# Gated graph network and graph attention on 64 graphs: one product in three passes, the end of the last graph in halves, and a new table of leads

## The chip, the core and the metric

The kernel runs on one core of a Trainium2 chip. The metric is device time in microseconds (us) from the start to the end of one execution. Time before the change: 1938.69 us, the median of three runs (1938.57 to 1942.45).

The core has several engines, each with its own queue of instructions. TensorE (PE in the profile) multiplies matrices: a weight load (LDWEIGHTS, shown as PEld) puts a 128 x 128 block into the array, and a matmul streams columns past it into a PSUM bank. VectorE (DVE), ScalarE (ACT) and GpSimd (POOL) work elementwise, SyncE (SP) issues the DMA transfers. An instruction starts when those ahead of it in its own queue have started and when the semaphores that it waits for are set.

## The reference

x holds 64 graphs of 256 nodes with 256 features each, adj the 64 adjacency matrices. Two layers, both behind a layer norm and a relu, are added to x:

```python
h = relu(layernorm(x))
A = (adj != 0)
for i in range(3):                        # gated network
    m = h @ weight[i]                     # per graph, 256x256 by 256x256
    aggr = A^T @ m                        # sum over the sources of each node
    r, z, n = GRU gates of (aggr @ w_ih.T + b_ih, h @ w_hh.T + b_hh)
    h = (1 - z) * n + z * h
x = x + h

h = relu(layernorm(x)) @ W.T              # graph attention
e = leaky_relu(h . a_left (rows) + h . a_right (columns), 0.2)
e = where(adj == 0, -1e9, e)
x = x + softmax(e) @ h
```

Everything is fp32, and so are the inputs and the output.

## The kernel before, in words

**Tiling.** Two graphs make a pair, so there are 32 pairs (`NPAIR`, `G` = 2), and most tiles are 128 partitions by 512 elements: 256 features or nodes in two blocks of 128 (`NB`, `DB` = 2), two graphs beside each other. In the gated network the features lie on the partitions, and the product of `weight[i]` with the input half of the gates is folded into one matrix per layer at the start (lines L680 and around), so a layer is a propagation by the adjacency matrix (L889) and then the gates.

**Three passes.** A product of fp32 tiles is made as a sum of three cheaper ones. `split16` (L718 to L726) splits one operand: ScalarE rounds it to a shorter fp32 form ("round", L718), VectorE subtracts that from the operand to get the remainder in 16 bits ("half", L720), and a scaled 16-bit copy of the operand is made too, by ScalarE if the operand lies in a bank (L723), else by VectorE (L726). The constant operand is split once at the start (`fac` for the rounded part, `low` for its 16-bit parts). The product is then fac x round, and two 16-bit products, summed in one bank. `limbs` (L736, L737) is the same split without the third copy, for the operand of the propagation. In the gates, `gate` (L750) issues six matmuls of 512 columns for each matrix: one in the fp32 form and two in 16 bits, for two blocks of features. The planner counts a change between the two forms as `SWITCH`, and `narrow` turns the order of the passes round, so that two products in a row meet in the same form.

**The gated step** of each block of 128 features, after the gates: tanh of r (L908), u (L913), u plus the n gate (L916), tanh (L918), tanh of z (L921), and three VectorE steps that give the new h (L925 to L929). L772 adds a bias to the gate nh. The new h is turned from features to nodes by the DMA's transpose (`dma_turn`: the transpose at L782, two gathers at L787) and put together by ScalarE (`join`, L795); in the first and the last pair TensorE turns it.

**Attention.** `norm_relu` (L810 to L823) makes the layer norm: statistics on VectorE, an epsilon (L815), a power on GpSimd (L817), a shift (L819), and two relus on ScalarE (L823). Then come products with a_left and a_right (L987), the row of right terms (by DMA, L996 and L999, or in the last two pairs by TensorE, L1008), the leaky relu (L1013), the mask (L1016), the row maximum (L1018), the exponentials with their sums (L1024), a scaling of the sums (L1032, `total`), the reciprocal (L1034), and the turn of the weights p. The order of products is then not the reference's: softmax(e) @ (h W^T) is made as (softmax(e) @ h) W^T. `mix` is the first product, in three passes up to pair 29 (L1053) and in plain fp32 in pair 30 (L1061); `project` is the one with W^T, in three passes up to pair 29 (L1072) and, in pair 30, in plain fp32 behind a copy of the bank (L1079, L1083). `out` (L1088) scales by the reciprocal and adds x, and one transfer of 256 KB stores the graph (L1091).

**The last pair** (31; `far` is false for it alone) does it the other way round: h is turned by TensorE (L1102), copied (L1105) and multiplied with W^T (L1110, copied at L1114). Then, for each graph and each block of 128 rows, come the exponentials (L1120), the reciprocal (L1123), the turn of p (L1128) and its copy (L1131), the product with the finished h W^T (`mix`, L1135: two matmuls of 256 columns in plain fp32), `out` (L1138) and a store of 128 KB (L1141).

**What sets the order.** Each operation is handed to a planner (`Plan`) with a name, its engine, an estimate of its time, and what it reads and writes. Buffers come from pools (28 "full", 22 "round", 40 "half", 8 PSUM banks and so on), and at most four pairs are open at a time. The planner gives each operation a priority, a due time less the latency of what follows, less its lead, and then again and again writes out the operation that can start first by its estimates, among equals the one with the lower priority value. The order on each engine's queue is thus fixed when the kernel is built. The leads are the table `LEAD`, one number per name; the prefixes "first", "pen", "late" and "last" name pairs 0, 29, 30 and 31, "of 0" and "of 1" the graphs of a pair where they are done one by one:

```python
o.stage, o.name, o.lead = self.stage, self.prefix + name, self.lead.get(name, 0)
if self.prefix:
    o.lead += self.lead.get(o.name, 0)
...
for o in self.ops:
    o.prio -= o.lead
...
if fits and (best is None or (t, o.prio, o.seq) < best[0]):
    best = ((t, o.prio, o.seq), o)
```

The diff's places in full, and what calls them:

Of the kernel before, what the change touches and what calls it, by code (L numbers as in the profile page):

```python
# [31 lines left out]
    "A": -600500, "A16": -500, "G 0": 165000, "G 1": 5500, "b_nh": 44500, "b_rz": -8000, "b_rz half": -20500,  # L32
    "back 0": -414000, "back 0 gather": -44000, "back 0 of 0": -9000, "back 0 of 1": -66000, "back 1": -646000,
    "back 1 gather": -4000, "back 1 of 0": 110000, "back copy 0": 188500, "back copy 1": 65500, "c0 0": 13500,
    "c0 1": -4000, "c0 d": 169000, "c1 0": -3500, "c1 1": 1000, "c1 d": 11000, "d add 0": 29000,
    "d add 0 of 1": -14500, "d add 1": 103000, "d add 1 of 0": 38500, "d mul 0": 21000, "d mul 0 of 0": 2000,
    "d mul 0 of 1": 35000, "d mul 1": 193000, "d mul 1 of 1": 1000, "d sub 0": -43000, "d sub 0 of 1": -20000,
    "d sub 1": -40000, "d sub 1 of 0": -13000, "d sub 1 of 1": -26000, "dot 0": 32000, "dot 1": 37000,
    "exps 0": -105000, "exps 0 0": -13000, "exps 0 1": -4000, "exps 1": 202000, "exps 1 1": 26500, "fill": 36000,
    "first A": -14500, "first A16": -18500, "first back 0": 107000, "first back 0 gather": 1500,  # L40
    "first back 1": -6500, "first back 1 gather": -15000, "first back copy 0": 76000, "first back copy 1": 16500,
    "first c0 0": 4000, "first c0 1": -20000, "first c0 d": 12000, "first c1 0": -14500, "first c1 1": 52000,
    "first c1 d": 43000, "first d add 0": 1000, "first d add 1": -14000, "first d mul 0": 1000,
    "first d mul 1": 29000, "first d sub 0": -16000, "first dot 0": 21000, "first dot 1": 2000,
    "first exps 0": -11500, "first exps 1": 36000, "first fill": 31000, "first g0 0": 16000, "first g0 d": 33000,
    "first g1 0": 38000, "first g1 1": 38500, "first g1 d": -116500, "first h0 0": 18500, "first h0 1": -263000,
    "first h1 1": 28000, "first hi 0": -30500, "first hi 1": 55500, "first in 0 eps": -60000, "first in 0 pow": 8000,
    "first in 0 relu": -11000, "first in 0 shift": 35500, "first in 0 stats": -201000, "first in 1 eps": -79500,
    "first in 1 pow": 21500, "first in 1 relu": 11500, "first in 1 shift": 57500, "first in 1 stats": 15500,
    "first in hi 0": 26500, "first in lo 0": 7500, "first in lo 1": -27000, "first leaky 0": 35500,  # L50
    "first line 0": 35000, "first line 1": -10500, "first lo 0": -500, "first lo 1": -7500, "first load": -5000,
    "first m0 1": 23500, "first m0 d": 3000, "first m1 0": 17000, "first m1 1": 3500, "first mask 0": 1000,
    "first mask 1": 5000, "first max 0": -4500, "first max 1": -5000, "first mid 0 eps": -14000,
    "first mid 0 pow": -32000, "first mid 0 relu": -49000, "first mid 0 shift": -6500, "first mid 0 stats": -69000,
    "first mid 1 eps": 98000, "first mid 1 pow": -8000, "first mid 1 relu": 88500, "first mid 1 shift": 9000,
    "first mid 1 stats": -90500, "first mix 0": -33000, "first nh 0 scale": 38000, "first nh 0 topF": -58000,
    "first nh 1 scale": 110000, "first nh 1 topF": 33000, "first ni 0 topF": 12000, "first ni 1 topF": 27500,
    "first out 0": -56500, "first p copy 0": -1000, "first p copy 1": 102000, "first p turn 0": 16000,
    "first p turn 0 gather": -25500, "first p turn 1": -5000, "first p turn 1 gather": 65500, "first p0 0": -16000,
    "first p0 1": 6500, "first p0 d": 17000, "first p1 0": -44000, "first p1 1": -4000, "first p1 d": -58500,  # L60
    "first project 0": -14000, "first prop 0": -8000, "first prop 1": 1000, "first r 0": 3500,
    "first r 0 topT": -42000, "first r 1": -57000, "first r 1 topF": 104000, "first recip": 10500,
    "first res 0": -50000, "first res 1": -16000, "first right 0": -10500, "first right 1": -122500,
    "first store": -16000, "first tanh 0": 41500, "first tanh 1": 4000, "first total": -3000, "first turn 1": -4500,
    "first turn copy 0": -5500, "first turn copy 1": 110500, "first u 0": -8000, "first u 1": -2000,
    "first u add 0": 25500, "first u add 1": 39500, "first w load full": -20000, "first z 0": 15500,
    "first z 0 topF": -14000, "first z 1": -13000, "g0 0": -41000, "g0 0 of 0": -59000, "g0 0 of 1": -29500,
    "g0 1": -26500, "g0 1 of 0": 1000, "g0 d": -97500, "g0 d of 0": 57000, "g0 d of 1": -14000, "g1 0 of 0": 28500,
    "g1 0 of 1": -9500, "g1 1": -5000, "g1 1 of 0": -128000, "g1 d of 1": -8000, "h copy 0": 27000, "h copy 1": 50000,
    "h turn 0": 9000, "h turn 1": -5500, "h0 0": -55500, "h0 0 of 0": -21000, "h0 0 of 1": 8000, "h0 1": -127000,  # L70
    "h0 1 of 0": -8000, "h0 1 of 1": -6000, "h0 d": -58500, "h0 d of 0": 50000, "h0 d of 1": 5000, "h1 0": 99500,
    "h1 0 of 0": -66500, "h1 0 of 1": 14000, "h1 1": 24500, "h1 1 of 0": 16000, "h1 1 of 1": 17500,
    "h1 d of 0": 51500, "h1 d of 1": 49500, "hW 0": 41500, "hW 1": -104000, "hW copy 0": -4000, "hi 0": 82000,
    "hi 0 of 0": 99000, "hi 0 of 1": 73000, "hi 1": -95500, "hi 1 of 0": 54500, "hi 1 of 1": 54000, "ident": -32500,
    "in 0 eps": 8000, "in 0 pow": 26500, "in 0 relu": 313500, "in 0 shift": 3000, "in 0 stats": 136000,
    "in 1 eps": 30000, "in 1 pow": -39500, "in 1 relu": 8000, "in 1 shift": -4000, "in 1 stats": 401500,
    "in hi 0": -175000, "in hi 1": 128000, "in lo 0": 30000, "last A": 56000, "last A16": 8000, "last back 0": 83500,
    "last back 0 of 0": 57500, "last back 0 of 1": 2000, "last back 1": 4000, "last back 1 of 0": -46500,
    "last d add 0": -8000, "last d add 0 of 0": -47000, "last d add 0 of 1": 6000, "last d add 1": -45000,
    "last d add 1 of 0": -8000, "last d add 1 of 1": -18000, "last d mul 0": -10000, "last d mul 0 of 0": -16500,  # L80
    "last d mul 0 of 1": -7000, "last d mul 1": -17500, "last d mul 1 of 0": -1000, "last d mul 1 of 1": -21000,
    "last d sub 0 of 0": -21000, "last d sub 0 of 1": -8000, "last d sub 1": 8000, "last d sub 1 of 0": -37000,
    "last d sub 1 of 1": -17000, "last dot 1": 48500, "last exps 0 0": 47000, "last exps 0 1": 138000,
    "last exps 1 0": 105000, "last exps 1 1": 3000, "last fill": 150000, "last g0 0": -8000, "last g0 0 of 0": 4500,
    "last g0 0 of 1": 1000, "last g0 1": 5500, "last g0 1 of 1": -2000, "last g0 d": -30500, "last g0 d of 1": 49500,
    "last g1 0": 53500, "last g1 0 of 0": 15500, "last g1 1 of 0": -9500, "last g1 1 of 1": -8000,
    "last g1 d": -33000, "last g1 d of 0": 153000, "last g1 d of 1": -23500, "last h copy 0": 13500,
    "last h turn 1": 6000, "last h0 0": 12000, "last h0 0 of 0": 146500, "last h0 0 of 1": -4000, "last h0 1": 70500,
    "last h0 1 of 1": 10000, "last h0 d": -8000, "last h0 d of 0": 2000, "last h0 d of 1": 65500, "last h1 0": 17000,
    "last h1 0 of 0": 8000, "last h1 0 of 1": 16000, "last h1 1": 7500, "last h1 1 of 0": -43000,  # L90
    "last h1 1 of 1": -13000, "last h1 d of 0": -16000, "last h1 d of 1": -15000, "last hW 1": 20500,
    "last hW copy 1": -81000, "last hi 0": -37500, "last hi 0 of 0": 4000, "last hi 0 of 1": 66000,
    "last hi 1": -4000, "last hi 1 of 0": 56500, "last hi 1 of 1": 24500, "last in 0 eps": -4500,
    "last in 0 pow": 6000, "last in 0 relu": 2000, "last in 0 shift": -44500, "last in 0 stats": -16000,
    "last in 1 eps": 5500, "last in 1 pow": -47000, "last in 1 relu": -63000, "last in 1 shift": -10500,
# [299 lines left out]
def tile_gated_gnn_then_gat(  # L395
# [77 lines left out]
    def parts(b):  # L473
        return b.t[:, :GN].rearrange("p (k d) -> p k d", k=2)
# [707 lines left out]
```

## Time and profile before

| | |
|---|---|
| median of three runs | 1938.69 us (1938.57 to 1942.45) |
| the profiled execution, its own time | 1937.01 us |
| its span, first to last instruction | 1935.2 us |
| TensorE's granted clock | 1.000 |
| plain fp32 product with W^T in pair 30 (L1083) | 16 records |
| three-pass product with W^T, all pairs up to 29 (L1072) | 4% of the chain |
| weight-load records | 10320, as many as matmuls |
| DMA | 240.25 MB, mean 124 GB/s |

The profile is one execution on the chip. A record of busy time belongs to one instruction. A matmul of plain fp32 leaves two records. The chain that ended last is followed back from the last instruction, at each step to what released it or to the instruction before it on its engine; its shares tell where the time of the span went. In a chain line the first number is the start in us, the second the length, then come the engine, the tile, the line and the number of instructions. In a line of TensorE's timeline, a group of matmuls is shown with start, length, line, the tile written and the tiles read, partitions and columns, and in brackets the idle time ahead of it and what ended it. "SPq" is SyncE's queue, "q" behind another engine's name likewise.

### The profile page before, as it was taken

To read this page: it belongs to the slowest core of one execution; us is meant where nothing else is said; L and a number is where in the kernel's file an instruction comes from. 1 tells how busy PE (TensorE), PEld (TensorE's weight loads), DVE (VectorE), ACT (ScalarE), POOL (GpSimd) and SP (SyncE) were. 2 spreads that over 40 slices of the span, in tenths; PEclk is the share of its full clock that TensorE was granted. 3 is DMA by queue.
4 is the path that set the end of the run, shared out by engine and by line. 5 is a ranking of instruction groups with operands and counts; after the bars stand their busy time and mean duration, and the time that the engine had idled before them with its cause. 6 is when DMAs were issued, how large, how long until landed. Compare 5 with 4: busy or idle time off the path is not lost.

```text
span 1935.2 us, 31695 instructions
## 1 busy us (share of the span) xinstructions
PE 1926.4 (100%) x10320; PEld 1215.5 (63%) x10320; DVE 1652.2 (85%) x3954; ACT 1608.7 (83%) x2798; POOL 196.8 (10%) x280
## 2 busy tenths in 40 slices
PE   9999999999999999999999999999999999999999
PEld 6556656666666666666666666666666666666668
DVE  7678888888888888898888898888988888888888
ACT  7668888888888888888888888888888888888876
POOL 3000101001011010110010110101100101100000
PEclk9999999999999999999999999999999999999999
DMA  4157766667756677766697566777666976666642
GB/s 142 34 109 131 140 130 123 124 124 140 142 124 118 121 146 137 137 116 124 123 142 145 123 118 122 140 137 140 122 115 123 147 140 125 125 123 133 118 77 67
DMA packets 738120, 240.25 MB, mean 124 GB/s; under 512 B 662160, under 2 KB 737952, under 8 KB 737952
## 3 DMA queue, kind: packets, MB, share of 16 engines
q1 hardware_dynamic: 737920, 238.20, 64.9%
q8 instruction: 81, 1.33, 0.3%
q14 instruction: 87, 0.71, 0.2%
q10 hardware_dynamic: 32, 0.01, 0.0%
HBM read 60.83 MB, written 16.84 MB: 40 GB/s over the span
## 4 chain that ended last, share of the span: by engine, by line
PE 94%; DMA 2%; ACT 2%; DVE 1%; SPq 1%; issue 0%; ACTq 0%; DVEq 0%
PE bank L750 76%; PE bank L889 9%; PE bank L1072 4%; PE bank L1053 4%; DMA full<-full 1%; SPq L787 1%; DMA x<-in_x_dram 0%; ACT round L718 0%; ACT full L795 0%; DMA line<-small 0%; DMA full<-line 0%; PE bank L680 0%; ACT half L723 0%; DVE half L720 0%; PE bank L1135 0%
## 5 line engine op out<-in xcount | busy, mean ns | idle before, releaser
L750 PE MATMUL bank<-half,low_hh 128*128 128x512 f16 (+1 forms) x2352 | 617.2, 376 | 0.0
L750 PE MATMUL bank<-half,low 128*128 128x512 f16 (+1 forms) x2352 | 616.6, 376 | 0.0
L750 PE MATMUL bank<-round,fac_hh 128*128 128x512 f32 (+1 forms) x1176 | 417.2, 441 | 0.0
L750 PEld LDWEIGHTS <-low 128*128 128x128 f16 x2352 | 213.5, 98 | 268.2 <-issue 53.3
L750 PE MATMUL bank<-round,fac 128*128 128x512 f32 (+1 forms) x1176 | 377.9, 419 | 0.0
L750 PEld LDWEIGHTS <-low_hh 128*128 128x128 f16 x2352 | 208.6, 98 | 258.9 <-issue 69.4
L795 ACT COPY full<-full 128x1024 uint16<-128x1024 uint16 x306 | 350.7, 1163 | 15.9 <-DMA full<-full 11.5
L817 POOL TENSOR_TENSOR small<-small,nhalf 128x2 f32<-128x2 f32 x128 | 116.6, 927 | 1507.3 <-DVE small L815 1505.9
L750 PEld LDWEIGHTS bank<-round,fac 128*128 128x128 f32 x1176 | 218.9, 189 | 60.2
L750 PEld LDWEIGHTS bank<-round,fac_hh 128*128 128x128 f32 x1176 | 213.7, 189 | 59.0
L720 DVE SCALAR_TENSOR_TENSOR half<-bank,round 128x512 f16<-128x512 f32 (+1 forms) x254 | 173.3, 683 | 38.0 <-ACT half L723 33.6
L772 ACT ACTIVATE bank<-bank,b_nh 128x512 f32<-128x512 f32 (+1 forms) x196 | 127.1, 649 | 86.2 <-PE bank L750 83.0
L908 ACT ACTIVATE full<-bank,b_rz 128x512 f32<-128x512 f32 (+1 forms) x196 | 132.4, 675 | 73.1 <-PE bank L750 72.7
L720 DVE SCALAR_TENSOR_TENSOR half<-full,round 128x512 f16<-128x512 f32 (+1 forms) x254 | 169.4, 677 | 6.8 <-ACT round L718 4.2
L913 DVE SCALAR_TENSOR_TENSOR full<-full,bank 128x512 f32<-128x512 f32 (+1 forms) x196 | 131.4, 670 | 47.7 <-ACT full L908 47.7
L918 ACT ACTIVATE full<-full,vec 128x512 f32<-128x512 f32 (+1 forms) x196 | 139.8, 713 | 38.9 <-DVE full L916 38.3
L921 ACT ACTIVATE full<-bank,b_rz 128x512 f32<-128x512 f32 (+1 forms) x196 | 132.2, 674 | 47.7 <-PE bank L750 47.4
L718 ACT ACTIVATE round<-full 128x512 fp32r<-128x512 f32 (+1 forms) x254 | 153.3, 627 | 21.0 <-DVE full L929 20.2
L718 ACT ACTIVATE round<-bank 128x512 fp32r<-128x512 f32 (+1 forms) x254 | 151.5, 598 | 17.3 <-PE bank L889 17.2
L916 DVE TENSOR_TENSOR full<-full,bank 128x512 f32<-128x512 f32 (+1 forms) x196 | 131.6, 672 | 28.5 <-PE bank L750 21.9
L737 DVE SCALAR_TENSOR_TENSOR half<-full,round 128x512 f16<-128x512 f32 x184 | 126.9, 691 | 33.9 <-ACT round L736 31.2
L723 ACT ACTIVATE half<-bank 128x512 f16<-128x512 f32 (+1 forms) x254 | 151.2, 597 | 2.9 <-DVE half L720 1.6
(126 smaller groups left out, 2539.8 us busy)
## 6 DMA issues: line engine op xcount, KB each, us to landing
full<-full SPq DMA_DIRECT2D x488, 128.0 KB, 3.6
x<-in_x_dram SPq DMA_DIRECT2D x64, 256.0 KB, 3.1
adj<-in_adj_dram SPq DMA_DIRECT2D x64, 256.0 KB, 4.1
full<-in_x_dram SPq DMA_DIRECT2D x64, 256.0 KB, 4.2
full<-full SPq DMA_DIRECT2D x248, 64.0 KB, 2.8
out_dram<-full SPq DMA_DIRECT2D x62, 256.0 KB, 2.3
full<-line SPq DMA_DIRECT2D x60, 128.0 KB, 3.4
full<-full SPq DMA_TRANSPOSE x306, 3.3
```

The lines of the kernel that those rows point to most:

```text
L718: act(f"{name} 0{of}", cut(A512 if bank else C512), lambda: nc.scalar.activation(v0.t[:, cols], v.t[:, cols], AF.Copy, scale=up), r=[(v, h ...
L720: dve_(f"{name} 1{of}", cut(V512), lambda: nc.vector.scalar_tensor_tensor(v1.t[:, cols], v.t[:, cols], up, v0.t[:, cols].bitcast(F32), op0 ...
L723: act(f"{name} d{of}", cut(A512), lambda: nc.scalar.activation(vd.t[:, cols], v.t[:, cols], AF.Copy, scale=up * unit), r=[(v, has)], w=[(v ...
L750: return [(j, lambda start, j=j, kb=kb: nc.tensor.matmul(bank.t[:, cols], fs(j, kb), s[kb][j].t[:, cols], start=start, stop=True, skip_gro ...
L772: act(name + " scale", fit(575, part), lambda: nc.scalar.activation(bank.t[:, cols], bank.t[:, cols], AF.Identity, bias=bias), r=[("b_nh", ...
L795: act(name, 1065, lambda: nc.scalar.copy(dst.t.bitcast(U16).rearrange("p (j n b) -> p j n b", j=2, b=2), src.t.bitcast(U16).rearrange(f"p ...
L889: nc.tensor.matmul(pa.t[:, ts(g, N)], b, m[:, ts(sb, N)], start=(n == 0), stop=True, skip_group_check=True)
L908: act(f"r {db}{of}", fit(575, part), lambda b=r_, k=pr, db=db, cols=cols: nc.scalar.activation(b.t[:, cols], k.t[:, cols], AF.Tanh, bias=b ...
L913: dve(f"u {db}{of}", fit(S512, part), lambda u=u, k=ph, b=r_, cols=cols: nc.vector.scalar_tensor_tensor(u.t[:, cols], b.t[:, cols], 1.0, k ...
L916: dve(f"u add {db}{of}", fit(V512, part), lambda u=u, k=pn, cols=cols: nc.vector.tensor_add(u.t[:, cols], u.t[:, cols], k.t[:, cols]), r=[ ...
L918: act(f"tanh {db}{of}", fit(615, part), lambda u=u, en=en, cols=cols: nc.scalar.activation(u.t[:, cols], u.t[:, cols], AF.Tanh, bias=b_i[: ...
L921: act(f"z {db}{of}", fit(575, part), lambda b=z_, k=pz, db=db, cols=cols: nc.scalar.activation(b.t[:, cols], k.t[:, cols], AF.Tanh, bias=b ...
```

## The change

It has three parts.

1. In pair 30 the product with W^T is made in three passes as in the pairs before it: the bank of the mix is split by `split16` with the factor `UP_V`, and the sums of the exponentials are scaled by `total`. The mix of pair 30 stays plain fp32.
2. In the last graph (graph 1 of pair 31) the mix, `out` and the store of each block of rows are made in two halves of 128 columns: four matmul groups, four VectorE steps and four stores of 64 KB in place of two each.
3. The table `LEAD` has other numbers for nearly all names, new ones for the halves, and so the planner writes another order on every engine.

```diff
 LEAD = {
-    "A": -600500, "A16": -500, "G 0": 165000, "G 1": 5500, "b_nh": 44500, "b_rz": -8000, "b_rz half": -20500,
...
+    "p copy 0": -104000, "p copy 0 0": -15500, "p copy 0 1": 4000, "p copy 1": 29000, "p turn 0": 5000,
...
 }
@@ -1028,7 +1030,7 @@
         for g in range(G if far else 0):
             sm = sms[g]
-            if p < NPAIR - 2:
+            if far:
                 dve("total", 70, lambda sm=sm: nc.vector.tensor_scalar(sm.t[:, 4 : 4 + NB], sm.t[:, 4 : 4 + NB], 1.0 / DOWN, None, op0=ALU.mult),
                     w=[(sm, (1,))])
@@ -1062,8 +1064,8 @@
                 pe(f"mix {g}", 4 * MM, mix, r=[(pT, ALL), (hb[g], ALL)], w=[(pg, ONE)])
-            if p < NPAIR - 2:
-                cs = split16(f"c{g}", pg, UP_V / (UP_H * UP_P), True)
+            if far:
+                cs = split16(f"c{g}", pg, UP_V / (UP_H * UP_P) if p < NPAIR - 2 else UP_V, True)
@@ -1130,16 +1132,21 @@
-            def mix(g=g, pT=pT, pv=pv):
-                for jb in range(NB):
-                    nc.tensor.matmul(pv.t[:, :D], pT.t[:, ts(jb, P)], parts(hW[g])[:, jb, :], start=(jb == 0), stop=(jb == NB - 1))
-
-            pe("mix" + name, 2 * MM, mix, r=[(pT, ONE), (hW[g], ONE)], w=[(pv, ONE)])
-            dve("out" + name, VP256, lambda b=XR[g], ib=ib, pv=pv, sm=sm: nc.vector.scalar_tensor_tensor(
...
-            dma("store" + name, 128, lambda g=g, ib=ib, b=XR[g]: nc.sync.dma_start(
...
+            for k, c in enumerate([slice(0, D)] if g < G - 1 else [slice(0, D // 2), slice(D // 2, D)]):
+                name_ = name + ("" if g < G - 1 else f" {k}")
+                part_of = ONE if g < G - 1 else (("half", k),)
+
+                def mix(g=g, pT=pT, pv=pv, c=c):
+                    for jb in range(NB):
+                        nc.tensor.matmul(pv.t[:, c], pT.t[:, ts(jb, P)], parts(hW[g])[:, jb, c], start=(jb == 0), stop=(jb == NB - 1))
+
+                wide = c.stop - c.start
+                pe("mix" + name_, 2 * MM * wide // D, mix, r=[(pT, ONE), (hW[g], ONE)], w=[(pv, part_of)])
+                dve("out" + name_, VP256 if wide == D else 240, lambda b=XR[g], ib=ib, pv=pv, sm=sm, c=c: nc.vector.scalar_tensor_tensor(
...
+                dma("store" + name_, wide // 2, lambda g=g, ib=ib, b=XR[g], c=c: nc.sync.dma_start(
...
         plan.due = None
```

## The prediction, made before the changed kernel was run

> **What bounds the kernel now.** I read the first two parts of the page, then the chain that ended last, then TensorE's waits, then the end of the timeline.
>
> ```profile
> span 1935.2 us, 31695 instructions
> PE 1926.4 (100%) x10320; PEld 1215.5 (63%) x10320; DVE 1652.2 (85%) x3954; ACT 1608.7 (83%) x2798; POOL 196.8 (10%) x280
> PE 94%; DMA 2%; ACT 2%; DVE 1%; SPq 1%; issue 0%; ACTq 0%; DVEq 0%
> ```
>
> TensorE is busy all the time and the chain is 94% TensorE. The Trainium skill warns of just this reading ("Perfetto Trace Analysis", Identifying the Most-Contended Engine): matmuls are pipelined, so busy time of the matmul row is a bad metric and the busy share of weight loads is a better one. That share is 63% here, which would leave up to 37% of TensorE's time (some 700 us) to be won by a better order. The chain decides which reading holds; each line is a start, a length and a group:
>
> ```profile
> 1086.82 16.02 PE bank L750 x72
> 1145.82 16.02 PE bank L750 x72
> 1204.82 16.02 PE bank L750 x72
> 1263.82 16.02 PE bank L750 x72
> ```
>
> 72 matmuls of 512 columns in 16.02 us are 0.2225 each, and the same place comes back every 59.00 us, pair after pair. A queue with gaps in it would not repeat to 0.01 us. So within a pair of graphs no order gains anything: the skill's rule would promise hundreds of us, the spacing says zero, and I take the spacing. What an order can win are the places where TensorE waits:
>
> ```profile
> 7.19 0.44 PE L642 MATMUL bank<-ident,full 128*128 128x128 f32 x2 [0.78 <-DMA full<-in_L_gnn_w_ih_dram]
> 13.13 0.77 PE L859 MATMUL bank<-ident,full 128*128 128x128 f32 x5 [0.16 <-ACT full L823]
> 218.24 0.61 PE L889 MATMUL bank<-half,half 128*128 128x256 bf16 x4 [0.45 <-DVE half L737]
> 233.13 1.03 PE L1053 MATMUL bank<-half,half 128*128 128x256 f16 x8 [1.25 <-DVE half L720]
> 1818.93 0.61 PE L889 MATMUL bank<-half,half 128*128 128x256 bf16 x4 [0.54 <-DVE half L737]
> ```
>
> The bracket is the idle time before the group and who ended it. With one more of 0.24 at 7.87 and the first 1.36 us, that is all up to the tail: 2.24 us in the body (0.45 + 1.25 + 0.54), 1.18 in the head besides the start.
>
> **The product in three passes.** In the chain, before and after stand side by side:
>
> ```profile
> 1822.28 2.71 PE bank L1072 x24
> 1920.67 3.45 PE bank L1083 x16
> ```
>
> L1083 is the product to be changed, two graphs in 16 records; L1072 is the same product, in three passes, of an earlier pair, 24 records for two graphs. 3.45 - 2.71 = 0.74 us less on TensorE. In exchange each graph needs two more ScalarE/VectorE steps: a copy of a bank twice (L718, L723) where L1079 copied it once, one subtraction (L720, 0.69), and a small scaling of sums (L1032, 0.17), which precedes a reciprocal that nothing waits for until the product is done.
>
> Queued behind these steps is the relu (L823) of the last graph, for which its turn (L1102) waits. Now the relu starts at 1921.71 on ScalarE, after two exponentials (L1120, 1.00 us from the first to the step behind them) and the copy L1114. In the changed order of instructions the exponentials stand after the relu. So ScalarE's 2 x 0.47 more (copies there follow at 1917.28 - 1916.81) fall into the time before 1920.7, when L1114 gets its product (ended about 1920.5), and the relu can follow at 1921.2. On VectorE its shift (L819), at 1920.34 now, gets two subtractions ahead of it (+1.38), but the maximum (L1018, 0.69) is moved behind it: 1921.0. The relu then takes 1.09 and ends at 1922.3, before TensorE reaches the turn: 1923.96 now, 1923.22 without 0.74. That 0.9 us is the cover; a relu later than 1923.2 would give the gain back microsecond for microsecond. Late next are the exponentials, at 1922.2 to 1923.2, read by the transposes L1128, which stand behind the turn anyway. The subtraction that the first product reads ends at about 1919.5, TensorE is free for it at 1920.5: nothing. So the whole -0.74 reaches the tail, where the chain goes L1083, L1102, L1105, L1110, L1135, one after the other.
>
> **Sums and stores of the last graph in halves.** The end of the path:
>
> ```profile
> 1929.69 2.01 PE bank L1135 x8
> 1931.73 0.48 DVE full L1138
> out_dram<-full SPq DMA_DIRECT2D x62, 256.0 KB, 2.3
> out_dram<-full SPq DMA_DIRECT2D x4, 128.0 KB, 1.7
> ```
>
> The last two lines are issues: number, size, us to landing. TensorE: 8 records of 256 columns at 0.216 (3.45/16) become 16 of 128 columns. The nearest row for narrow records of this type is L697 in the chain of the head, 8 in 0.79 us with only 2 columns, so about 0.10 to 0.11 is what a weight load allows, the same as 128 columns at half of 0.216. I take 0.11: 1.76 for 1.73, +0.03; at the worst the recorded length of the load, 0.19, is the spacing: +1.3. VectorE: L1138 takes 0.48 on 256 columns; the same operation costs 0.68 on 512 and 0.42 on 256 elsewhere (L913), 0.26 for 256 columns, so half costs 0.35: -0.13. Store: 2.3 for 256 KB and 1.7 for 128 KB make 0.6 per 128 KB, so 64 KB land 0.3 earlier. Against that stands a rule of the skill ("DMA: Bandwidth & Descriptors", Anatomy of one DMA): some 2 us per transfer are fixed and the bytes go at 436 GB/s, by which 64 KB less gain 0.15. It is fitted to another issuing path; the two rows are of this one, so -0.3. The queue: four stores leave SP instead of two. The three weight loads at 2.25 take 1.49, 0.50 each; the gathers of the chain (L787) take 0.60 to 0.65. The four halves come off VectorE 0.45 us apart, so the last is sent 3 x 0.5 = 1.5 (to 1.9) after the first where its data are ready at 1.35: +0.15 to +0.55. Sum: +0.03 - 0.13 - 0.30 + 0.25 = about -0.15; by the skill's figure 0. Ends: -0.4 and +1.4. Nothing is queued behind these stores.
>
> **The new leads** shift the whole order. TensorE's rows are otherwise the same in number and kind, the 27 idle-filling and warming transposes of the head too; changes between fp32r and 16-bit passes go from 1344 to 1350 for the product. A pair has 59.00 us less the sum 56.3 of its records at 0.2133 per 512 columns, for some 42 changes: 0.06 each, inside the 2.71 for the product's own. In the repeated pairs the new order only swaps neighbours (one six-matmul gate goes ahead of a propagation L889, another comes between the two halves of a reset gate), so 59.00 stays. At the three body waits:
> - 218.24: a gate of six matmuls (1.33 us) now stands before this propagation; the wait was 0.45. Gone unless its producer is later too.
> - 233.13: the waiting mix now has 1.34 us more TensorE work ahead of it, and its gather, at present the fifth of five in SP's queue (L787 from 219.93 to 226.9, 1.3 us each), goes ahead of one of them. The wait was 1.25. Gone.
> - 1818.93: the low half (L737) that is late was ready to be made from 1805.3 but stood behind ten ScalarE steps; it is now made right after its relu. But the propagations are also 2.7 us earlier in TensorE's order. I count nothing, between -0.54 and +2.
> Together -1.7. In the head the weight products (L680) come earlier and the turn of the first graphs (L859) 3.5 us later; the 0.16 goes, but ScalarE (9.79 of 10 us busy from 10 to 20) and VectorE (9.02) feed those products, and up to 1 us of wait can come in its place. I take 0, between -0.9 and +1.
>
> **Sum** against the profiled execution, 1937.01 with a span of 1935.2: -0.74 - 0.15 - 1.7 = -2.6, a span of 1932.6, execution 1934.4. The median of the runs, 1938.69, is 1.68 above the profiled one, so 1936.1.
>
> **Rivals.**
> - The edits alone (0.20): other waits of the same size take the place of those removed. -0.9, 1937.8. For it: three such waits in 1930 us are what an order made from estimates may leave again. Against: the positions above.
> - All waits go (0.22): -0.74 - 0.15, body -2.24, and in the head -0.34 (its share of 10 to 20 us in which TensorE is not busy) and part of the 0.78: -4.2, 1934.5. For it: the producers have moved as well as the consumers. Against: the two loads of w_ih are issued as before, so the 0.78 is a DMA's.
> - Slower (0.08), one mechanism: a repeated pair gets a wait. The thinnest cover is at the third propagation of a group: its low half (L737) runs 1106.00 to 1106.68 and the propagation starts at 1107.2, 0.5 us later. If the new order makes that half later by d, each of some 25 repeated pairs loses d - 0.5. To undo the -2.6 and to be 0.2% slower takes 6.5/25 = 0.26 us each, d = 0.76, hardly more than one VectorE step (0.69): 1943 and more. Against: there the four L737 now stand together, ahead of an L720 that was between them, so d is negative.
>
> **From cases to numbers.** Likeliest (0.50): 1936.1, its own range 1934.9 to 1937.6. About 0.2%, 3.9 us, is what a measurement of this kernel can tell from no change: faster means below 1934.8, slower above 1942.6. The case of all waits gone lies just below that line, the first two above: faster 0.22, same 0.70, slower 0.08. The range 1934.0 to 1939.6 leaves out the slower case and small tails of the others.
>
> **What would show it.** L1083 gone and 24 more records of the three-pass product in its place, two graphs in 2.7 us; h's turn right behind them, 0.7 us earlier than now; four stores of 64 KB landing in 1.4 us, 0.5 apart; no wait at about 217 and 232; the chain's repeat still 59.00. It is wrong if the repeat is 59.1 or more, if a wait over 1 us stands in the head or near 1815, or if the narrow records are 0.19 apart.

## The result, and the profile after

The changed kernel takes 1935.39 us (median of ten runs, 1934.52 to 1937.20), the kernel before 1938.62 us in the same session (ten runs, 1935.98 to 1943.37). The ratio is 0.9978, 95% interval 0.9970 to 0.9985. In a second session, with the changed kernel built again, it was 1935.21 us (21 runs) against 1937.34 (65 runs), ratio 0.9991 (0.9985 to 0.9998). So the gain is 2 to 3 us in 1938; forecast were 2.6 and a time of 1936.1.

The profiled execution of the changed kernel is its slowest of the ten, 1937.20 us with a span of 1935.4, which is 0.2 longer than the span shown of before. Read alone, this one profile would say that nothing was gained. That is why the stretches below are compared over several executions. The first two parts of its page, and the shares of the chain:

```profile
span 1935.4 us, 31827 instructions
...
PE 1925.9 (100%) x10336; PEld 1223.2 (63%) x10336; DVE 1654.1 (85%) x3960; ACT 1607.7 (83%) x2800; POOL 197.8 (10%) x280
...
PE 92%; DVE 3%; DMA 3%; ACT 2%; issue 1%; SPq 0%; DVEq 0%; ACTq 0%
```

TensorE is still busy throughout, with 16 more matmul records (8 for the product, 8 for the halves). Its weight loads have gone from 1215.5 to 1223.2 us, and nothing follows from that. The chain of the repeated pairs (start, length, group):

```profile
539.02 2.71 PE bank L1074 x24
...
598.02 2.71 PE bank L1074 x24
...
657.02 2.71 PE bank L1074 x24
...
716.02 2.71 PE bank L1074 x24
```

The three-pass product comes back every 59.00 us, as before: the new leads change nothing within a pair. TensorE's waits, apart from the one at the very start (start, length, group, and in brackets the idle time ahead and who ended it; lines up to the last edit are two higher than before):

```profile
7.76 0.44 PE L644 MATMUL bank<-ident,full 128*128 128x128 f32 x2 [0.85 <-DMA full<-in_L_gnn_w_ih_dram]
...
8.47 0.66 PE L644 MATMUL bank<-ident,full 128*128 128x128 f32 x4 [0.27 <-DMA full<-in_L_gnn_w_ih_dram]
...
11.63 0.44 PE L682 MATMUL bank<-round,round 128*128 128x384 f32 x1 [1.03 <-ACT round L662]
...
25.12 0.66 PE L861 MATMUL bank<-ident,full 128*128 128x128 f32 x4 [0.44 <-DVE half L722]
...
1785.51 0.61 PE L891 MATMUL bank<-half,half 128*128 128x256 bf16 x4 [0.61 <-ACT full L825]
...
1818.89 1.03 PE L1055 MATMUL bank<-half,half 128*128 128x256 f16 x8 [1.01 <-DVE half L722]
```

The waits at 218 and 233 are gone and no wait stands in their place. At the end of the body 1.62 us of wait stand where 0.54 stood, and in this execution the head waits 1.4 us longer (2.59 for 1.18). The end of the chain:

```profile
1919.73 1.73 PE bank L1112 x8
1921.45 2.72 PE bank L1074 x24
1924.17 0.45 PE bank L1104 x4
1924.62 0.02 issue
1924.64 0.02 ACTq L1107
1924.66 0.04 issue
1924.70 0.59 ACT full L1107
1925.29 0.04 issue
1925.34 1.99 PE bank L1112 x8
...
1929.74 2.07 PE bank L1141 x16
1931.81 0.02 issue
1931.83 0.35 DVE full L1145
```

The product takes 2.72 instead of 3.45, and h's turn (L1104) follows at once. From the first L1112 to the last mix (L1141) are 10.01 us; in before, from 1918.95 to 1929.69, 10.74. From the last mix to the end of the span are 5.67 us, in before 5.53. The issues of the last graph's stores (number, size, us to landing):

```profile
out_dram<-full SPq DMA_DIRECT2D x2, 128.0 KB, 1.7
out_dram<-full SPq DMA_DIRECT2D x4, 64.0 KB, 1.6
```

### The profile page after: what moved, and what is told of

It reads as the page before. It is cut to its first block, busy times and chain, and to the rows that moved or that the text cites. A ratio compares the mean times of both kernels' runs of the same rounds, so it can differ in the third digit from the quotient of the medians.

```text
span 1935.4 us, 31827 instructions
## 1 busy us (share of the span) xinstructions
PE 1925.9 (100%) x10336; PEld 1223.2 (63%) x10336; DVE 1654.1 (85%) x3960; ACT 1607.7 (83%) x2800; POOL 197.8 (10%) x280
## 4 chain that ended last, share of the span: by engine, by line
PE 92%; DVE 3%; DMA 3%; ACT 2%; issue 1%; SPq 0%; DVEq 0%; ACTq 0%
PE bank L752 74%; PE bank L891 8%; PE bank L1074 4%; PE bank L1055 4%; DMA full<-full 2%; ACT full L797 0%; DVE half L722 0%; DMA line<-small 0%; DVE full L915 0%; DMA full<-in_L_gnn_w_ih_dram 0%; DVE small L812 0%; ACT round L720 0%; DMA x<-in_x_dram 0%; DVE full L989 0%; PE bank L682 0%
## 5 line engine op out<-in xcount | busy, mean ns | idle before, releaser
L929 DVE SCALAR_TENSOR_TENSOR full<-full,full 128x512 f32<-128x512 f32 (+1 forms) x196 | 132.2, 674 | 25.7 <-ACT full L923 25.0
```

What stands on the lines that cost most here:

```text
L929: dve2(f"d mul {db}{of}", fit(V512, part), lambda d=d, b=z_, cols=cols: nc.vector.scalar_tensor_tensor(d.t[:, cols], b.t[:, cols], 1.0, d. ...
```

## The experiments

Ten runs were made, of nine kernels. Their times are medians; the kernel before stood at 1937.34, 1937.24 and 1937.36 us beside the three groups of runs.

**The changed kernel once more.** No edit.

> The changed kernel once more, unchanged, for a second look at one execution: its profiled one had a span of 1935.4 us, 1.8 above what its median run has. Theory A, the loads at the start decide how one execution differs from the next: then an execution nearer the median (span about 1933.5) has its three-pass product of the last pair but one not at 1921.45 but about 1.8 us earlier, and the difference is there already in the first 30 us (first wait for w_ih below 0.85 us, the product L682 that starts at 11.63 earlier). Theory B, the difference lies in the body or in the last store: the same product stands within 0.3 us of 1921.45 and the span differs behind it, or the two waits of 0.61 (L891 at 1785.5) and 1.01 (L1055 at 1818.9) are not there. Time by either: 1935.4, within 1 us.

Measured: 1935.21 us; the profiled execution 1934.20, its span 1932.4, 3.0 less than that of the first. All of TensorE's waits in it, but the one at the start:

```profile
14.52 0.44 PE L682 MATMUL bank<-round,round 128*128 128x384 f32 x1 [0.25 <-ACT round L662]
...
1815.89 1.03 PE L1055 MATMUL bank<-half,half 128*128 128x256 f16 x8 [0.88 <-DVE half L722]
```

Matmul for matmul this execution is 2.3 us ahead of the first one by 12 us and 2.7 by 25, of 3.0 at the last matmul. Of the rest, the wait at 1785, which is absent, gives 0.57 us; gaps near 1766, each too short for the timeline to show, take 0.49 of it back. Theory A holds for most of it: in the new order, executions differ in the first 25 us, where w_ih lands without a wait or with 1.1 us of it, and where the wait at the second L682 is 1.03 or nothing.

**Both edits with the old leads.** The table of before in the changed code, with the leads of the wholes for both halves:

```diff
 LEAD = {
-    (the new table)
+    (the table of before; "mix 1 0 0" and "mix 1 0 1" take the lead of "mix 1 0", and so on)
 }
```

> Both edits of the code with the old table of leads (the halves take the leads of the wholes). All engines have the order of before up to the last 20 us. My theory (terms of the sum add): -0.74 for the product and -0.15 for the halves, so 0.9 us under before; h's turn behind the product at 1923.3 to 1923.5 where before has 1924.13, and waits of 0.45, 1.25 and 0.54 us in the body as before. Rival 1 (the edits need the new leads): with the old leads the relu of the last graph is late, TensorE waits between the product and h's turn, and the time is that of before or up to 1 us over it. Rival 2 (the edits are the whole gain, the leads nothing): 3 to 4 us under before.

Measured: 1939.49 us, ratio to before 1.0013 (1.0007 to 1.0020): slower. The timeline of its tail (lines are one higher than in the changed kernel):

```profile
1923.45 0.60 ACT L826 ACTIVATE full<-full,small 128x256 f32<-128x256 f32 x1 [0.65 <-DVE small L822]
...
1924.36 1.99 PE L1142 MATMUL bank<-full,full 128*128 128x256 f32 x8 [0.26 <-ACT full L1134]
...
1926.19 0.60 PE L1105 MATMUL bank<-ident,full 128*128 128x128 f32 x4
...
1927.52 1.99 PE L1113 MATMUL bank<-wT,full 128*128 128x256 f32 x8 [0.51 <-ACT full L1108]
...
1930.74 0.93 PE L1131 MATMUL bank<-ident,full 128*128 128x128 f32 x4 [1.23 <-ACT full L1123]
```

Rival 1 holds, though the time is 2.1 us over before where it had said at most 1. The last relu (L826) starts at 1923.45, behind the exponentials and behind a late shift (L822), h's turn (L1105) comes only at 1926.19, behind the mix of the other graph, and what then waits for it stands bare: 0.26, 0.51 and 1.23 us. The prediction had named this price, a relu later than 1923.2; it needs the new leads to stay unpaid.

**The new leads with the old code.**

```diff
 LEAD = {
-    (the table of before)
+    (the new table; "mix 1 0" takes the lead of "mix 1 0 0", and so on)
 }
```

> The old code with the new table of leads (the wholes take the leads of the first halves); all engines have the order of the changed kernel up to the last 20 us. My theory: the leads give 1.7 us by the two body waits that go (at 218 and 233), less what the new waits at 1785 and 1818 take (1.62 for 0.54), less or more what the head does; with the result of -3.2 us for the whole and 0.9 for the edits, 2.3 us under before. Rival 1 (the profile's own ledger: the head of the changed kernel loses about what the body gains): within 0.5 us of before. Rival 2 (the leads are the whole gain): 3 to 4 us under before.

Measured: 1936.39 us, ratio 0.9996 (0.9987 to 1.0004), 0.95 under before by the medians. The waits at 218 and 233 are absent here too. In the tail two new ones stand (the lines are those of before):

```profile
1926.76 1.99 PE L1110 MATMUL bank<-wT,full 128*128 128x256 f32 x8 [0.73 <-ACT full L1105]
...
1929.76 1.99 PE L1135 MATMUL bank<-full,full 128*128 128x256 f32 x8 [0.57 <-ACT full L1131]
```

From the first L1110 (1918.02 in the chain) to the last mix are 11.74 us, 1.0 more than before, so the leads are worth more in head and body than the time shows. Neither 2.3 nor within 0.5 nor 3 to 4, and the interval does not tell it from no gain. Each half of the change alone spoils the tail, the edits by 2 us, the leads by 1.

The four kernels of this group show that the parts do not add: before 1937.34, the edits alone 2.15 over it, the leads alone 0.95 under it, both together 2.13 under it. With the old leads the edits cost 2.15 us; with the new ones they gain 1.18 (1936.39 to 1935.21).

**Both edits with the new leads in the tail alone.** The old table, but in the last pair's attention and in the product ahead of it each name's whole lead (its own and its prefix's) is that of the new table; 98 entries differ from those of the kernel with the old leads, by this rule:

```diff
 LEAD = {
+    (the table of before, and "last X" = new "X" + new "last X" - old "X" for X among the steps of the attention;
+     likewise "late X" for the sums, the split, the product and the store of pair 30)
 }
```

> Both edits on the order of before for all but the last 20 us; in those, the attention of the last pair and the product of the pair before it take their leads from the new table, so that TensorE has the changed kernel's order there (h's turn right behind the product). With the old leads throughout, the same edits made the last relu late (L823 of before at 1923.45) and lost 2.2 us. My theory (that order is all that the edits need): no wait between the product and h's turn, the stretch from the start of the last three-pass product (or whole product) to the end of the span as in the changed kernel, 13.95 us, where before has 14.5 from its product; about 0.65 us under before (1936.7 for 1937.3), waits of 0.3 to 0.5 at 218, 0.9 to 1.3 at 233 and 0.5 at 1819 as before. Rival (the edits need the whole table): a wait of 0.5 us or more among the last products, and the time within 0.3 us of before or over it.

Measured: 1937.50 us, ratio 0.9999 (0.9991 to 1.0007). TensorE's timeline:

```profile
1819.48 0.61 PE L899 MATMUL bank<-half,half 128*128 128x256 bf16 x4 [0.54 <-DVE half L747]
...
1923.22 0.73 PE L1082 MATMUL bank<-fac_W,round 128*128 128x256 f32 x4
1923.78 0.60 PE L1112 MATMUL bank<-ident,full 128*128 128x128 f32 x4
...
1929.51 2.05 PE L1149 MATMUL bank<-full,full 128*128 128x128 f32 x16
```

h's turn (L1112) follows the product with no wait. By the timelines' starts, from the first product with W^T (1919.34) to the last mix are 10.17 us; before has 10.91 in its second trace (1920.51 to 1931.42). That is the predicted 0.74. But the time does not show it, because from the last mix to the end are 6.32 us, 0.8 more than before. The half-way expectation of 0.65 therefore failed at the stores and not at the order. The waits of the body are those of before (0.15, 1.09, 0.65 and 0.54).

**The halves undone.**

```diff
-            for k, c in enumerate([slice(0, D)] if g < G - 1 else [slice(0, D // 2), slice(D // 2, D)]):
+            for k, c in enumerate([slice(0, D)]):
```

Each whole takes the lead of its first half.

> The changed kernel with the mix, the sum and the store of the last graph whole again; every other instruction stands where it stood. The prediction's term was -0.15 for the halves, so undoing them should cost 0.15. The two profiles of the changed kernel say the opposite: from the first matmul of the last mix to the end of the span 5.66 and 5.69 us, where before had 5.51. Theory A (the halves lose): 5.5 us in that stretch, 0.15 faster in the span; in the time too little to tell, within 0.5 us of the changed kernel. Theory B (the term as predicted): 5.8 us.

Measured: 1935.05 us; from the last mix to the end 5.18 us (1927.06 to 1932.24), where the changed kernel has 5.67, 5.66 and 5.67 in three traces. The chain has

```profile
1927.06 2.01 PE bank L1139 x8
1929.09 0.48 DVE full L1143
```

where the changed kernel has 2.07 and 0.35. Theory A holds, and with a larger price than I had read off: the halves lose 0.48 in the traces. In the time (1935.21 and 1935.05) so little cannot be told. Two other kernels with whole stores and the new order end in 5.18 too.

**A bank for each half.**

```diff
                 part_of = ONE if g < G - 1 else (("half", k),)
+                if k > 0:
+                    pv = Buf("bank")
```

> The changed kernel with a bank of its own for each half of the last mix. Theory (both halves of a bank were announced by one signal of TensorE, so that the first sum waited for the second half too): the sums start 0.45 us apart, the first at 0.75 us behind the first matmul of the last mix where the changed kernel has 1.2, the last sum takes 0.35 us alone instead of ending 0.61 behind the first, and the stretch from that matmul to the end is 5.4 us, 0.25 under the changed kernel and 0.1 under before. Rival (the stores' issue sets the end: four at 0.47 us each): the stretch stays within 0.1 us of 5.66. Time within 0.5 us of the changed kernel by either.

Measured: 1934.83 us, and from the last mix to the end 5.16 us, 0.5 under the changed kernel. VectorE's timeline of the changed kernel, where both halves lie in one bank:

```profile
1930.94 0.61 DVE L1145 SCALAR_TENSOR_TENSOR full<-bank,small,full 128x128 f32<-128x128 f32 x2 [1.22 <-PE bank L1141]
1931.83 0.61 DVE L1145 SCALAR_TENSOR_TENSOR full<-bank,small,full 128x128 f32<-128x128 f32 x2 [0.28 <-PE bank L1141]
```

And with two banks:

```profile
1928.75 1.69 DVE L1147 SCALAR_TENSOR_TENSOR full<-bank,small,full 128x128 f32<-128x128 f32 x4 [0.78 <-PE bank L1143]
```

With one bank the sums come in twos, the first two 1.2 us behind the start of the mix (1929.74): the first of them waited for the matmuls of the second half as well. With two banks the first comes at 0.75 us and all four run in one row. SyncE's stores of this graph in the changed kernel, with the halves undone, and with two banks (start of the first to end of the last issue):

```profile
1928.74 4.33 SPq L1148 DMA_DIRECT2D out_dram<-full  x6
...
1926.06 3.87 SPq L1146 DMA_DIRECT2D out_dram<-full  x4
...
1927.01 3.88 SPq L1150 DMA_DIRECT2D out_dram<-full  x6
```

With one bank the last issue ends 3.33 us behind the start of the mix, with whole stores 2.87, with two banks 2.89. The four halves are still issued some 0.46 apart, but from 1.13 us on instead of 1.58, so the rival fails. The first part of the expectation holds; the end is 0.24 better than the 5.4 expected. Against whole stores (5.18) the halves gain 0.02 even so.

**The kernel before once more.**

> The kernel before, unchanged, for a second look at one execution of it. By the theory that executions differ in the first 30 us, its three-pass product near 657 us stands up to 1.5 us from 657.25, with waits of 0.3 to 0.5 and 0.9 to 1.3 us at 218 and 233, and the tail from 1888.2 on is 47.0 us long within 0.2. Rival: the difference between executions stands in the body or the tail.

Measured: one run, 1938.74 us, span 1937.0. The product is at 658.42 instead of 657.25, and the difference is not in the first 30 us: a wait of 1.11 us at 191.81 and one of 0.17 at 193.06 were not in the first trace. At 1818.35 there is one of 0.44 more, which both kernels with the edits on the old order of the body have too (0.64 and 0.65). The tail is 47.04 long. The numbers of the expectation came out, but its theory failed and the rival holds: the old order has more places in the body that wait in some executions.

**Seven operations issued elsewhere.** The planner's order is kept, and the instructions are issued from a list in which some are moved behind others (the expectation says eight; there are seven):

```diff
-            o.fn()
+            emit.append((o.name, o.pair, o.fn))
...
+MOVES = [
+    (("fill", 1, 0), ("A16", 1, 1)),      # name, pair, which; moved behind the second
+    (("fill", 1, 0), ("A16", 1, 1)),
+    (("fill", 2, 0), ("A16", 1, 1)),
+    (("fill", 2, 0), ("A16", 1, 1)),
+    (("pen lo 0", 29, 1), ("m0 1", 28, 0)),
+    (("p1 0", 28, 0), ("p copy 1", 28, 0)),
+    (("p1 1", 28, 0), ("p1 d", 28, 0)),
+]
```

> The changed kernel with eight operations issued at other places in their queues, nothing else moved: the four GpSimd memsets of pairs 1 and 2 (L984 at 9.08 to 11.0 us) go behind the casts of pair 1 at about 38 us; one low half (L739 of pair 29) goes ahead of four steps on VectorE; and the rounding and the remainder of one p (L720, L722 of pair 28) go ahead of those of a bank. Theory A (each of these stands at the end of a wait of TensorE): a VectorE step of 128x6 elements no longer takes 1.89 us and the one behind it 1.81 us at 9.1, the wait of 1.03 us at 11.63 goes, so do those of 0.61 and 1.01 at 1785.5 and 1818.9: 2.6 us under the changed kernel, about 1932.8. Rival 1 (the memsets are not the cause, the steps wait for something else): the two VectorE steps are as long as before, 1.6 us under. Rival 2 (the work behind is late instead: waits of like size just behind the three places): within 0.5 us of the changed kernel.

Measured: 1935.26 us, the same as the changed kernel (1935.21). The moves removed what they were aimed at in two places of three, and gained nothing in sum. The step on b_rz takes 0.17 us, so its cause was the memsets; the wait of 1.03 at the second product of the head is gone, one of 0.34 stands at 15.70, and w_ih came late in this execution (1.24 us of wait). The wait at 1785 is gone, but one of 0.35 stands at 1813.71. At 1818 the wait is as long as it was, though the remainder of p, which ended it in the changed kernel, now ends at 1817.09, a microsecond ahead:

```profile
1816.40 0.69 DVE L744 SCALAR_TENSOR_TENSOR half<-full,round 128x512 f16<-128x512 f32 x1 [0.24 <-ACT round L742]
1817.38 0.69 DVE L744 SCALAR_TENSOR_TENSOR half<-bank,round 128x512 f16<-128x512 f32 x1 [0.28 <-ACT half L747]
```

The mix (at 1818.12) now waits for the second of these, the remainder of a bank, until 1818.07. The mix had two conditions, and the profile of the changed kernel could name only the later one. In the planner's list the bank that this remainder reads is the one that the mix writes. Rival 2 holds, by the time and at this wait; in the other two places the new waits are smaller than the old ones.

**The best of the order tried, and the two banks again.** The halves undone and the first five of the moves together; and the kernel with two banks once more.

> What the runs point to as the best of the order tried: the changed kernel with the last graph's mix, sum and stores whole, the four memsets of pairs 1 and 2 behind the casts at 38 us, and the low half of pair 29 ahead of four steps on VectorE. Theory (three terms add): the end from the last mix's first matmul 5.2 us where the changed kernel has 5.67, so -0.5; no wait of 1.0 at the second L680 in the head, which two of five traces of this order with the memsets in place showed, so -0.4 in the mean; no wait at 1784, which two of six showed (0.61 and 0.26), so -0.15: 1934.2 where the changed kernel has 1935.2. Rival (the head is set by when the loads land, whatever VectorE does): -0.5 alone, 1934.7.

> The changed kernel with a bank for each half, once more, beside the whole version with the moved steps on the same chip. Theory: the end from the last mix's first matmul 5.16 us again, as short as with whole stores (5.18), so 0.5 under the changed kernel, 1934.7; its head keeps the memsets, so in an execution in which they start between 8.9 and 9.1 us a VectorE step of 128x6 elements takes 0.9 us or more. Rival (the 5.16 was one execution's): 5.4 or more.

Measured: 1934.75 us (ratio to before 0.9988, 0.9980 to 0.9996) and 1935.04 (0.9989, 0.9982 to 0.9995). The ends are 5.18 and 5.16 us as expected. The first is 0.5 under the changed kernel, which is the rival's 1934.7: the moves in the head gave nothing that the times show. A gain of 0.5 is less than these intervals can tell, so what is shown is the shorter end in the traces, not a faster kernel.

## Why the prediction was right

**The ledger of the traces.** The body's waits are all waits of TensorE from 180 to 1900 us. "Head" is the start of the three-pass product of the repeated pairs near 657 us less the waits from 180 to 240. "Tail" is from the first product with W^T in the chain to the last mix, "end" from there to the end of the span. The two kernels with moved instructions are left out.

| trace | order of the body | body's waits | head | end |
|---|---|---|---|---|
| before, first and second | old | 2.24, 3.84 | 655.55, 655.57 | 5.53, 5.54 |
| edits, old leads; edits, tail leads | old | 2.48, 2.43 | 655.47, 655.53 | 6.44, 6.32 |
| changed, first and second | new | 1.62, 0.88 | 657.02, 654.24 | 5.67, 5.66 |
| leads only; no halves | new | 1.35, 0.88 | 655.22, 654.88 | 5.18, 5.18 |
| two banks, twice | new | 0.84, 1.48 | 655.68, 655.40 | 5.16, 5.16 |

Means: body's waits 2.75 in the old order and 1.18 in the new, -1.57; head 655.53 and 655.41, -0.12. For tail and end, before and the changed kernel alone: 10.74 and 10.01, -0.73; end +0.13. Sum -2.3, against -2.1 and -3.2 measured by medians. Nothing else moved: from the product near 657 to the first product with W^T, less the waits between, are 1261.31 us in the old order and 1261.33 in the new (means; 1261.08 to 1261.59).

**Repeated pairs (59.00 us, no gain).** Right.

**The product (-0.74).** Right, -0.73, with the cover as described: the relu ahead of h's turn.

```profile
1922.29 1.09 ACT L825 ACTIVATE full<-full,small 128x256 f32<-128x256 f32 x2 [0.16 <-DVE small L821]
```

It ends at 1923.38 and the turn is at 1924.17, 0.8 us of cover where 0.9 were foreseen. The experiment with the old leads shows what the same edits cost where that cover is missing.

**The body's waits (-1.7).** Right in sum, at two places of three for the named reasons. At 218 and 233 the old order waits 1.2 to 1.7 us in four traces (2.85 with the place at 192 in one), the new order not at all. In the first trace of the changed kernel the halves that were late end at 220.12 and at 233.54 at the latest, and the propagation and the second mix start at 221.04 and 234.50, so each is covered by some 0.9 us, as named. The prediction did not see that the passes come in the other order there, fp32 first: the 16-bit pass, which reads the half, starts only at 221.51 and 234.98, another 0.48 of cover. At 1818.93 I counted nothing: the wait of 0.54 at the propagation went, and one of 0.78 to 1.01 at the mix (L1055) came in every trace of the new order without the moves. That it would come was not seen; the range of -0.54 to +2 held it.

**The head (0, between -0.9 and +1).** Right as a mean (-0.12, with some 0.4 of uncertainty by the spread of six), but that spread was not foreseen. Four traces of the old order agree within 0.1 us, six of the new differ by 2.8. Part of this is a step that the prediction did not cost. Four GpSimd memsets (L984), issued in one row in the new order, run beside a VectorE step of 6 columns; VectorE and GpSimd in the changed kernel and in its second two-bank trace:

```profile
9.08 1.92 POOL L984 MEMSET full<- 128x512 f32 x4
...
9.14 1.89 DVE L579 TENSOR_SCALAR b_rz<-b_rz 128x6 f32<-128x6 f32 x1
```

```profile
8.48 1.94 POOL L984 MEMSET full<- 128x512 f32 x4
8.54 1.42 DVE L579 TENSOR_SCALAR b_rz<-b_rz 128x6 f32<-128x6 f32 x1
```

With the memsets elsewhere:

```profile
8.97 0.17 DVE L601 TENSOR_SCALAR b_rz<-b_rz 128x6 f32<-128x6 f32 x1
```

**The halves (-0.15).** The step that failed, in sign: in the same order they cost 0.48. Of its terms, by the records of the end: the narrow matmuls +0.05 (+0.03 foreseen: they are 0.11 apart, as taken). VectorE +0.13 instead of -0.13, since both halves of a bank were waited for together, so that two sums of 0.35, overlapping to 0.61, stand behind the last matmul where one of 0.48 stood. The queue +0.23 (+0.15 to +0.55 foreseen): the stores are issued 0.47 apart, the last at 2.95 us behind the start of the mix where the whole one goes at 2.54. The landing -0.12 instead of -0.30, from 1.71 to 1.6: here the rule of the Trainium skill ("DMA: Bandwidth & Descriptors", Anatomy of one DMA), a fixed part and bytes, by which 64 KB less gain an estimated 0.15, was nearer than my extrapolation from the 256 KB row. And +0.2 for what the sum had left out, SyncE's last waits, one after another behind the landing. The VectorE and the queue term have one cause: with a bank for each half the last sum ends 2.44 us behind the start of the mix and the last store is issued at 2.50, and the end is 5.16. Against before only +0.13 of the 0.48 is seen, because with whole stores the old order ends in 5.53 where the new one ends in 5.18. The prediction did not foresee these 0.35, and that they hide most of the miss is luck.

**Time.** -2.6 from the profiled execution, and the median 1.68 above it, gave 1936.1. The ledger gains 0.3 less than that sum, about what the halves were off. The 1.68 did not last: beside 65 runs of before the median was 1937.34, 0.33 above that profiled execution. With it the sum would have said 1934.7, 0.5 under the 1935.21 that came, where 1936.1 was 0.9 over it. So the time came out close by a gain 0.5 too large and an offset 1.35 too large, which partly cancel; that is luck. Two of the prediction's signs of being wrong appeared in the profiled execution, a wait over 1 us in the head and one near 1815. The second stands in every trace of the new order without the moves, at 0.78 to 1.01, and is the term that was counted at nothing. The first is 1.03 here beside 1.12 of late w_ih, in the slowest of the ten executions; the first trace with two banks has 1.02 and no late w_ih, and its time is near its median.

**What stays open.** Why the end is 0.35 (whole) to 0.7 us (halves) longer with the old order of the body. The last sum ends at the same distance from the mix (2.52 whole, 2.70 in halves); SyncE's steps come later. The four traces of the old order have an instruction load among the transfers behind 1925 us,

```profile
q14 instruction: 1, 0.01, 0.2%
```

and the traces of the new order have none. This goes with the delay but was not tried; in the first trace of before the load starts only at 1934.9, behind SyncE's late step at 1934.3, so that step did not wait for the transfer shown. Open too is whether moving the memsets helps: both traces with them moved had late loads of w_ih (waits of 1.2 and 1.6 us), and the times do not tell.

## What to carry to other kernels

Where one engine is bound and its order repeats exactly, count what its waits add up to: that sum is all that a new order can win, and here it was won to some 60% with nothing gained inside a pair. An edit at the end of a kernel is only worth its own sum in an order in which nothing late stands behind it: the same two edits lost 2.15 us in one order and won 1.18 in another. Before a transfer or a sum is cut into halves, see whether the halves can be read apart, and add the issue of each piece to the sum; here they gained 0.02 us even apart.

## What the hardware showed that was not expected

A VectorE step of 6 columns waited out a whole number of memsets: 0.49 us in one trace, 0.94 and 0.95 in two, 1.42 in one, 1.88 and 1.89 in two, that is one, two, three or four memsets of 0.47, and 0.17 with none beside it. In each of these traces the step ends within 0.03 us of the end of a memset. The Trainium skill ("SBUF — State Buffer", Who interferes with whom) says that VectorE in a 2-port mode, which a `tensor_scalar` such as this step can enter, and GpSimd contend for a shared pair of ports, and that whoever issues first has it for the whole instruction while the other blocks. The traces agree with that, though none shows the mode of the step, and add that the step does not always get its turn when the first memset ends. TensorE's wait at the second L682 follows it: 1.03 and 1.02 us with four memsets, 0.68 with three, at most 0.22 with two or one.

One profiled execution can mislead about a change of 0.15%: the changed kernel's two have spans of 1935.4 and 1932.4 us.
